# The chained factors of the two hyperbolic layers: a rewritten chain, and a last stage in two groups of tiles

## The chip, the cores and the metric

The kernel runs on one core of one Trainium2 chip. The metric is the device time of one execution in microseconds. An execution was also profiled by the hardware: the profile lists every instruction of the five engines (TensorE: PE for matmuls and PEld for weight loads; VectorE: DVE; ScalarE: ACT; GpSimd: POOL; SyncE: SP, which here only starts DMAs), with start and duration, the program line it comes from, and the names of what it writes and reads. "L720" is line 720 of the program before the change. Times in the profile count from the first instruction.

## The reference

Four graph layers on 3327 nodes with 64 features and a sparse 0/1 matrix `adj`. Each layer normalizes `x`, takes the positive part, and adds its result to `x`. Layers 0 and 3 are the hyperbolic ones. Their core, cut to what matters here:

```python
h = jnp.maximum(_layernorm(x), 0.0)
adj_att = sigmoid(left[:, None] + right[None, :] + b) * adj       # 3327 x 3327
x_local = logmap(h[:, None, :], h[None, :, :], c)                 # mobius_add(-p1, p2), artanh of its norm
support = einsum('ij,ijd->id', adj_att, x_local)
second  = tanh(0.5 * sqrt_c * lambda_x(h, c) * norm(support)) * support / (sqrt_c * norm(support))
res     = mobius_add(h, second, c)                                # num / max(den, 1e-15)
x       = x + where(norm(res) > maxnorm, res / norm(res) * maxnorm, res)
```

`x_local` is never built. All of it lies in the plane of two vectors, so per node the layer's result is `ah * Xr + am * M`: `Xr` is the scaled input row, `M` the row summed over the neighbours, and `ah` and `am` are two numbers per node. They follow from a handful of numbers per node by a long chain of elementwise steps: two square roots, a tanh, two or more divisions. This chain is called the factors below.

Layer 1 is a weighted sum over the last neighbours of each row (counts along a row, exponentials of them, then a product with the features); layer 2 is an attention with two GRU cells.

## The kernel before

**Tiles.** The 3327 nodes are padded to 26 tiles of 128. A number per node is a 128x26 tile, features are 128x26x64. The two halves of the 26 tiles (0 to 12 and 13 to 25) are handled side by side: a chunk `(t, n)` means tiles t to t+n-1 of both halves. `by_tiles(t, c)` is that view of a tile.

**The loops of layers 0 and 3** (`hyperbolic_series`). The columns come in four chunks, `(0, 4), (4, 3), (7, 3), (10, 3)`; each chunk goes over the 26 row blocks, which makes K = 104 steps, two of them to each turn `j` of the loop at L684. A step is: PE products (L611, L612), ACT arctan (L617), ACT sigmoid (L598), POOL times the adjacency (L600), DVE `weights` (L621), PE `sums` (L630, L638). What ends a chunk is put into the dictionary `later` and done in the next turns: `out_of` (ACT copies the sums, L648), `back` (PE transposes them, L657), `to_m` (DVE product for `hm`, L667; ACT square for `mm`, L668) and `to_m2` (DVE sum `M0`, L673; ACT copy to `M`, L674; DVE sum `hm`, L676; then DVE sum `mm`, L677). `M0`, `hm` and `mm` are the numbers per node from which the factors start.

**Order.** ACT, DVE, PE and POOL have their order written out by hand inside a region (L579) that starts before the loop. In layer 0 it stays open until the end of layer 1, so the factors and all of layer 1 run in the order in which they are written. In layer 3 it is closed after the loop (L815); from there a scheduler orders the instructions. SP's DMAs are in the order of their issue.

**After the loop of layer 0**, `plain_decay` begins layer 1. It runs the first count steps of layer 1 (PE counts L1467, ACT exponentials L1473) ahead of the normalization: one of them (`ahead_of_norm(0)`) before `to_m`, one after it, then `e.factors(tp)` (L1620), then eight more. The DVE adds `ah * Xr + am * M` to `X` tile by tile (L1520) and normalizes four groups of tiles (L1525 to L1555), which gives the parts `h` that PE needs for the sums of layer 1 (L1481).

**After the loop of layer 3** all 26 tiles take the factors at once, then `X` is updated in two halves of 13 tiles (L817 to L833): for each half DVE makes two products (L830; the last one is made by ACT tile by tile, L823) and two adds (L831), and `done` starts the half's store (L1956).

**The factors** (`factors`, L713 to L809) are some 63 DVE instructions on 128x26 numbers and one ACT tanh. `root_by_bits` (L122) gives 1/sqrt by a bit trick and three Newton steps of three instructions each. The quotient `1/d` is taken in the middle and multiplied into `am` and `ah` before the second norm. In layer 3 `um` is a lower bound on the tanh's argument.

**The end.** `ok` collects what shows that the fast path may be used: the count of nodes with `x2 >= X2_MIN` (L562, L563) and of adjacency values that are 0 or 1. PE sums it (L2003), DVE turns it into 0 or 1 in `badi` (L2004 to L2006), and every engine loads that number and branches over a slow path (L2007) that isn't taken.

Of the kernel before, what the change touches and what calls it, by code (L numbers as in the profile page):

```python
# [21 lines left out]
P = 128  # L22
# [12 lines left out]
X2_MIN = 22.0  # L35
ARTANH_CLIP = 0.5 * math.log((2.0 - 2.0 ** -23) * 2.0 ** 23)
# [12 lines left out]
def tile_gnn4(ctx: ExitStack, tc: tile.TileContext, x, adjT, att0, b0, w1, bias1, w_gat, a_gat,  # L49
# [72 lines left out]
    def root_by_bits(y, q, src):  # L122

        V.tensor_scalar(y.bitcast(I32), src.bitcast(I32), -0.5, float(0x5f375a86), op0=OP.mult, op1=OP.add)
        for _ in range(3):
            V.scalar_tensor_tensor(q, y, -0.5, y, op0=OP.mult, op1=OP.mult)
            V.tensor_mul(q, q, src)
            V.scalar_tensor_tensor(y, q, 1.5, y, op0=OP.add, op1=OP.mult)
# [171 lines left out]
    def ball(att, b_att, r, min_norm, min_norm2, after=None):  # L300
# [15 lines left out]
        cc, sqc, isqc, um, maxn2 = [const.tile([P, 1], F32, name=n + k) for n in ("cc", "sqc", "isqc", "um", "maxn")]  # L316
        if r is None:
            for t, value in ((cc, 1.0), (sqc, 1.0), (isqc, 1.0), (um, 0.0), (maxn2, min_norm2)):
                V.memset(t, value)
        else:  # L320
# [5 lines left out]
            def of_r():  # L326
                G.tensor_tensor(cc, cc, cc, op=OP.mult)
                for i, (to, src) in enumerate(((cc, cc), (sqc, cc), (isqc, cc))):
                    G.tensor_tensor(to, src, half[:, i:i + 1], op=OP.pow)
                G.tensor_scalar(um, sqc, min_norm / MIN_NORM, None, op0=OP.mult)  # L330
                G.tensor_scalar(maxn2, cc, min_norm2, None, op0=OP.mult)
            after.append(of_r)
        return wlr, bcol, cc, sqc, isqc, um, maxn2

    def hyperbolic_series(r, params, ok, masks=None, done=None, ahead=None, then=None, checks=None):
# [18 lines left out]
        with ExitStack() as st:  # L354
# [8 lines left out]
            wlr, bcol, cc, sqc, isqc, um, maxn2 = params  # L363
# [51 lines left out]
            with room(name="hsp", bufs=1) as tp, room(name="hsps", bufs=2, space=PSUM) as ps, \  # L415
# [136 lines left out]
                for o, (to, on) in enumerate(((junk, V), (pe, A))):  # L552
# [5 lines left out]
                    if o == 0:  # L558
# [3 lines left out]
                        V.scalar_tensor_tensor(good, x2, X2_MIN, nodes, op0=OP.is_ge, op1=OP.mult)  # L562
                        V.reduce_sum(ok, good, axis=AX.X)  # L563
# [96 lines left out]
            def to_m(j, c, slot):  # L660
# [4 lines left out]
                else:  # L665
                    prod = wk.tile([P, 2, 2, 4, D], F32, name="prod", bufs=1)[:, :, :, :c[1], :]
                V.tensor_mul(prod[:, 0], by_tiles(Xr, c), pm)  # L667
                A.activation(prod[:, 1], pm, AF.Square)  # L668
                later[j + 1, 0] = lambda: to_m2(j + 1, c, slot, pm, prod)

            def to_m2(j, c, slot, pm, prod):
                pm0 = slot[:, 1, :c[1] * P].rearrange("p (t i o d) -> p o t i d", i=2, o=2, d=32)
                V.reduce_sum(by_tiles(M0, c), pm0[:, :, :, :, 0], axis=AX.X)  # L673
# [5 lines left out]
            def at(k, first):  # L679

                return tiles[k][0] if 0 <= k < K and tiles[k][1] == 0 and tiles[k][0][0] >= first else None

            sigmoid(0)
            for j in range(-1, K // 2 + (5 if then is None else 1)):  # L684
# [3 lines left out]
                for i in range(2):  # L688
# [13 lines left out]
                    if i == 1 and (j, 1) in later:  # L702
                        later.pop((j, 1))()
                if at(2 * j + 10, 1):
                    columns(at(2 * j + 10, 1))
# [7 lines left out]
            def factors(tp):  # L713

                def new(name):
                    return tp.tile([P, T], F32, name=name)

                def mul(name, a, b):
                    o = new(name)
                    V.tensor_mul(o, a, b)  # L720
                    return o


                k1, k2, bx, bk2, bh, rr = [small[n] for n in ("k", "kb", "bx", "bk", "bh", "rr")]
                stt = V.scalar_tensor_tensor
                V.tensor_scalar(hm, hm, 0.5 * PF, None, op0=OP.mult)

                ca = mul("ca", M0, k2)
                w = mul("w", mm, bk2)
                V.tensor_sub(ca, hm, ca)  # L730
                u = mul("u", bx, hm)
                cx = mul("cx", ca, x2)
                v2 = new("v2")
                V.tensor_add(v2, cx, u)
                vh = new("vh")
                stt(vh, u, 0.5, cx, op0=OP.mult, op1=OP.add)
                V.tensor_mul(v2, v2, ca)
                V.tensor_add(v2, v2, w)
                th, t, a1, d, y2 = [new(n) for n in ("th", "t", "a1", "d", "y2")]
                ah, am = new("ah"), new("am")  # L740


                if r is None:


                    f = MIN_NORM
                    by, g = new("by"), new("g")
                    V.tensor_scalar(by, v2, -f * f, 1.0, op0=OP.mult, op1=OP.add)
                    V.tensor_scalar(g, by, MIN_NORM, None, op0=OP.max)
                    V.reciprocal(g, g)  # L750
                    V.tensor_mul(t, root, g)
                    A.activation(th, t, AF.Tanh)
                    V.tensor_mul(th, th, rr)
                    V.tensor_mul(y2, th, th)
                    stt(vh, vh, 2.0 * f, th, op0=OP.mult, op1=OP.mult)
                    V.tensor_mul(y2, y2, x2)
                    stt(d, v2, f * f, y2, op0=OP.mult, op1=OP.mult)
                else:

                    V.tensor_scalar(t, v2, 1e-8, None, op0=OP.max)  # L760
                    ti, tq = new("ti"), new("tq")
                    root_by_bits(ti, tq, t)
                    V.tensor_mul(t, t, ti)
                    V.tensor_scalar(t, t, um, None, op0=OP.max)
                    A.activation(th, t, AF.Tanh)
                    V.reciprocal(ti, t)
                    ta, th = th, new("th_t")
                    V.tensor_mul(th, ta, ti)
                    V.tensor_mul(y2, th, th)
                    stt(vh, vh, 2.0, th, op0=OP.mult, op1=OP.mult)  # L770
                    V.tensor_mul(y2, y2, v2)
                    V.tensor_mul(d, y2, x2)
                stt(d, d, 1.0, vh, op0=OP.add, op1=OP.add)
                stt(a1, vh, 1.0, y2, op0=OP.add, op1=OP.add)
                V.tensor_scalar(d, d, MIN_NORM, None, op0=OP.max)
                if r is None:
                    stt(ah, a1, f, ca, op0=OP.mult, op1=OP.mult)
                    V.reciprocal(d, d)
                    V.tensor_mul(by, by, th)
                    stt(am, a1, f, bx, op0=OP.mult, op1=OP.mult)  # L780
                    V.tensor_add(ah, ah, by)
                else:
                    V.tensor_mul(th, th, bx)
                    V.reciprocal(d, d)
                    V.tensor_mul(ah, th, ca)
                    V.tensor_mul(am, th, bx)
                    V.tensor_add(ah, ah, a1)
                V.tensor_mul(am, am, d)
                V.tensor_mul(ah, ah, d)

                hm_ = mul("hm_", hm, am)
                n2 = mul("n2", ah, x2)
                V.tensor_mul(am, am, k1)
                V.tensor_add(n2, n2, hm_)
                m2 = mul("m2", mm, am)
                V.tensor_mul(n2, n2, ah)
                V.tensor_mul(m2, m2, am)
                V.tensor_mul(ah, ah, bh)
                V.tensor_add(n2, n2, m2)
                if r is not None:  # L800
                    V.tensor_scalar(am, am, isqc, None, op0=OP.mult)
                V.tensor_scalar(n2, n2, maxn2, None, op0=OP.max)
                ns, nq = new("ns"), new("ns_q")
                root_by_bits(ns, nq, n2)
                n2 = ns
                V.tensor_scalar(n2, n2, 1.0 - 0.004, 1.0, op0=OP.mult, op1=OP.min)
                V.tensor_mul(am, am, n2)
                V.tensor_mul(ah, ah, n2)
                return ah, am  # L809

            if then is not None:
                then(SimpleNamespace(Xr=Xr, M=M, slots=slots, later=later, factors=factors, close=lp.close,
                                     ahead=ahead, close_all=hs.close))
                return
            region.close()  # L815
            lp.close()
            with room(name="hse", bufs=1) as tp:  # L817
                ah, am = factors(tp)
                last = HALVES[1]
                extra = tp.tile([P, T // 2, D], F32, name="extra")  # L820
                for k in range(T // 2):
                    t = last.start + k
                    A.activation(extra[:, k, :], M[:, t, :], AF.Copy, scale=am[:, t:t + 1])  # L823
                for ts in HALVES:
                    for a, b in ((Xr, ah), (M, am)):
                        if ts is last and a is M:
                            prod = extra
                        else:
                            prod = tp.tile([P, T // 2, D], F32, name="prod", bufs=2)
# [1223 lines left out]
```

## Time and profile before

| what | value |
|---|---|
| median of three runs (lowest to highest) | 730.57 us (729.93 to 732.24) |
| the profiled execution: its own time, and its span | 730.23 us, 728.5 us |
| busy share of the span: PE, DVE, ACT, POOL | 87%, 74%, 74%, 59% |
| mean granted TensorE clock | 0.961 of full speed |
| DMA | 119.25 MB, 164 GB/s over the span |
| chain that ended last, by engine | PE 64%, DVE 12%, issue 6%, POOL 6%, ACT 5%, DMA 4% |

The busy shares are means over stages with different limits. The chain that ended last is followed back from the last instruction: at each step to what released it, or to the instruction before it on its engine. The span runs from the first to the last instruction; about 1.7 us of the execution's own time lie outside it.

### The profile page before, as it was taken

To read this page: it belongs to the slowest core of one execution; us is meant where nothing else is said; L and a number is where in the kernel's file an instruction comes from. 1 tells how busy PE (TensorE), PEld (TensorE's weight loads), DVE (VectorE), ACT (ScalarE), POOL (GpSimd) and SP (SyncE) were. 2 spreads that over 40 slices of the span, in tenths; PEclk is the share of its full clock that TensorE was granted. 3 is DMA by queue.
4 is the path that set the end of the run, shared out by engine and by line. 5 is a ranking of instruction groups with operands and counts; after the bars stand their busy time and mean duration, and the time that the engine had idled before them with its cause. 6 is when DMAs were issued, how large, how long until landed. Compare 5 with 4: busy or idle time off the path is not lost.

```text
span 728.5 us, 11966 instructions
## 1 busy us (share of the span) xinstructions
PE 632.3 (87%) x4227; PEld 256.4 (35%) x4227; DVE 542.6 (74%) x999; ACT 536.7 (74%) x691; POOL 430.8 (59%) x326
## 2 busy tenths in 40 slices
PE   0899999999999798989998997169999999999940
PEld 0622233333333243434445642042223333333310
DVE  6867778777787799999645339887667877777656
ACT  2688888888888785687871586258888889888831
POOL 2699999989999202116620000048887887888820
PEclk9999999999999999999999999579999999999985
DMA  3988898898888706489940000203334444444001
GB/s 63 334 259 279 263 274 256 279 298 261 267 260 273 274 26 226 132 289 358 403 162 2 1 1 1 94 19 93 94 94 133 115 117 138 120 118 116 2 3 50
DMA packets 61494, 119.25 MB, mean 164 GB/s; under 512 B 9552, under 2 KB 33776, under 8 KB 61424
## 3 DMA queue, kind: packets, MB, share of 16 engines
q1 hardware_dynamic: 57072, 118.38, 51.1%
q10 hardware_dynamic: 4352, 0.02, 0.3%
q8 instruction: 35, 0.57, 0.3%
q14 instruction: 35, 0.29, 0.1%
HBM read 115.64 MB, written 0.88 MB: 160 GB/s over the span
## 4 chain that ended last, share of the span: by engine, by line
PE 64%; DVE 12%; issue 6%; POOL 6%; ACT 5%; DMA 4%; SPq 1%; ACTq 1%; POOLq 0%; DVEq 0%
PE slot L630 16%; PE slot L638 9%; PE slot L611 9%; PE slot L1467 8%; PE slot L612 7%; POOL sig L600 6%; PE slot L1766 5%; PE slot L1481 5%; DMA adj<-in 3%; ACT sig L598 2%; PE slot L1882 1%; DVE X L1520 1%; ACTq L307 1%; DMA own<-in 1%; DVE sig L621 1%
## 5 line engine op out<-in xcount | busy, mean ns | idle before, releaser
L621 DVE SCALAR_TENSOR_TENSOR sig<-slot,sig 128x768 f32<-128x768 f32 (+1 forms) x208 | 212.7, 1023 | 105.7 <-POOL sig L600 105.6
L617 ACT ACTIVATE slot<-slot 128x768 f32<-128x768 f32 (+1 forms) x208 | 177.3, 853 | 53.3 <-PE slot L612 53.0
L600 POOL TENSOR_TENSOR sig<-adj,sig 128x768 f32<-128x768 f32 (+1 forms) x104 | 201.1, 1960 | 14.5 <-ACT sig L598 11.5
L598 ACT ACTIVATE sig<-leftB,right 128x768 f32<-128x768 f32 (+1 forms) x208 | 203.3, 977 | 0.1
L600 POOL TENSOR_TENSOR sig<-mask,sig 128x768 f32<-128x768 fp8e4 (+1 forms) x104 | 173.2, 1678 | 40.5 <-ACT sig L598 35.1
L630 PE MATMUL slot<-sig,Xr 128*64 128x384 f32 (+1 forms) x832 | 169.3, 526 | 5.8 <-DVE sig L621 5.7
L611 PE MATMUL slot<-XC,XT 128*128 128x384 f16 (+1 forms) x416 | 142.2, 342 | 3.1 <-ACT sum L648 1.7
L612 PE MATMUL slot<-XF,XE 73*128 73x384 f16 (+1 forms) x416 | 141.4, 340 | 0.0
L638 PE MATMUL slot<-sig,X 128*32 128x384 f32 (+1 forms) x832 | 94.2, 525 | 0.0
L1473 ACT ACTIVATE w<-slot,ebias 128x832 bf16<-128x832 f32 x76 | 69.0, 952 | 26.3 <-PE slot L1467 25.9
L630 PEld LDWEIGHTS slot<-sig,Xr 128*64 128x64 f32 x832 | 49.8, 135 | 87.1 <-issue 62.0
L611 PEld LDWEIGHTS <-XT 128*128 128x128 f16 x416 | 40.7, 98 | 93.8 <-issue 67.4
L1467 PE MATMUL slot<-mask,rest 128*128 128x416 fp8e4 x208 | 53.9, 341 | 5.7 <-ACT adj L1473 3.5
L1467 PE MATMUL slot<-mask,after 128*128 128x416 fp8e4 x208 | 53.4, 339 | 1.3 <-DVE deg L1491 1.3
L612 PEld LDWEIGHTS <-XE 73*128 73x128 f16 x416 | 40.7, 98 | 29.5 <-issue 5.4
L1362 DVE TENSOR_SCALAR_CACHE_REDUCE same<-late 128x832 fp8e4<-128x832 f32 x48 | 48.4, 1009 | 0.0
L204 POOL TENSOR_TENSOR mask<-mask,offdiag 128x128 fp8e4<-128x128 fp8e4 x26 | 16.5, 645 | 46.1 <-PE slot L1467 46.1
L421 POOL MEMSET X<- 128x832 f32 x2 | 1.6, 792 | 69.4 <-DVE o L1911 69.4
L1766 PE MATMUL slot<-mask,own 128*64 128x416 fp8e4 x416 | 39.8, 346 | 2.2 <-DVE deg L1491 2.2
L638 PEld LDWEIGHTS slot<-sig,X 128*32 128x32 f32 x832 | 16.4, 108 | 67.7 <-issue 66.1
L1481 PE MATMUL slot<-w,h 128*64 128x416 bf16 x304 | 34.0, 345 | 0.0
L527 PE MATMUL pt<-ident_h,Xp 128*64 128x128 f16 x32 | 2.6, 313 | 35.5 <-ACT Xp L466 35.5
(323 smaller groups left out, 681.0 us busy)
## 6 DMA issues: line engine op xcount, KB each, us to landing
adj<-in SPq DMA_DIRECT2D x78, 384.0 KB, 4.8
late<-in SPq DMA_DIRECT2D x48, 416.0 KB, 3.2
adj<-in SPq DMA_DIRECT2D x17, 832.0 KB, 8.4
adj<-in SPq DMA_DIRECT2D x27, 512.0 KB, 5.1
ahead<-in SPq DMA_DIRECT2D x14, 832.0 KB, 6.4
ahead<-in SPq DMA_DIRECT2D x16, 416.0 KB, 5.6
own<-in SPq DMA_DIRECT2D x16, 416.0 KB
own<-in SPq DMA_DIRECT2D x8, 832.0 KB
```

The lines of the kernel that those rows point to most:

```text
L598: A.activation(sig, leftB[c], AF.Sigmoid, bias=right[:, b:b + 1])
L600: G.tensor_tensor(sig, adj, sig, op=OP.mult)
L611: PE.matmul(L[:, o, :c[1] * P], XT[:, rows], XC[c][:, o, :], start=True, stop=False)
L612: PE.matmul(L[:, o, :c[1] * P], XE[:KE, rows], XF[c][:, o, :], start=False, stop=True)
L617: A.activation(L, L, AF.Arctan, scale=PA / SX ** 2)
L621: V.scalar_tensor_tensor(sig, slot[:, :, :tiles[k][0][1] * P], PC, sig, op0=OP.add, op1=OP.mult)
L630: PE.matmul(acc[c][o * D:(o + 1) * D, 0, :n], Xr[:, b, :], sigs[k][:, o, :], start=b == 0, stop=b == T - 1)
L638: PE.matmul(acc[c][q:q + 32, 1, :n], X0[:, b - 1 + i, :], w[:, o, :], start=b == 1, stop=b == T - 1, tile_position=(0, q))
L1467: PE.matmul(cnt[o][:, h, :BK], w, cols(k, o, h), start=w is after and steps[k][1] == T - 1, stop=True, skip_group_check=True)
L1473: A.activation(ws[k][:, o, :, :], cnt[o][:, :, :BK], AF.Exp, scale=-LN2, bias=ebias)
L1481: PE.matmul(acc[c][o * D:(o + 1) * D, h, :BK], parts[i][:, b, :], w[:, o, h, :], start=b == T - 1 and i == 0, stop=b == 0 and i == 1)
L1766: PE.matmul(acc[k][o * D:(o + 1) * D, :], w, mask[:, o * HP + k * BK:o * HP + (k + 1) * BK], start=n == 0 and i == 0, stop=n == T - 1 and ...
```

## The change

1. **The chain is rewritten** for both layers. `root_by_bits` takes one third-order step and one Newton step in place of three Newton steps (8 instructions, before 10); constants are left out of the steps and multiplied in later (`ROOT`). The scaling of `hm` by 0.5·PF goes into the instructions that use it. `1/d` is no longer multiplied into `am` and `ah` before the second norm; the norm's bound is multiplied by `d` squared instead (`dd`), and `1/d` is taken as the upper bound of the last factor. In layer 3 the lower bound `um` is applied to the square (`um2`, with 1e-8 in it), so the tanh's argument needs no bound of its own and no reciprocal.
2. **The factors become a generator** that gives way after each instruction and works on a chunk's view. Layer 0 runs it to the end on all 26 tiles (`all_factors`). In layer 3 it runs once for the chunk `(0, 10)` of 20 tiles, "early", and once for the chunk `(10, 3)` of the last 6 tiles, "late". Eight early steps are written after each of the two `sigmoid` places of turn `j = K // 2`, where the loop has no more steps for DVE: 16 in all. The rest alternates with the late steps, one by one, and after the early factors the 20 tiles' X update takes their turn; then comes the late X update. The intermediate numbers lie in a part of a load buffer of the loop (`checks.adjs[2]`).
3. **The X update** (`moves`) lets ACT scale all of `M` in place, tile by tile, and DVE scale `Xr` in place and do both adds, in pieces of 5 tiles (early) and 3 tiles (late). `store_tiles` stores 20 tiles, then 6; each store takes two blocks of a partition.
4. The region of the written-out order now ends after all of this.
5. In `to_m` the DVE sum `M0` is written directly after the product, ahead of ACT's square, for every chunk of both layers.
6. A second condition, `x2 <= X2_MAX`, is one more DVE instruction in the preparation of both loops.

```diff
-    def root_by_bits(y, q, src):
+    def root_by_bits(y, q, r, src):
         V.tensor_scalar(y.bitcast(I32), src.bitcast(I32), -0.5, float(0x5f375a86), op0=OP.mult, op1=OP.add)
-        for _ in range(3):
-            V.scalar_tensor_tensor(q, y, -0.5, y, op0=OP.mult, op1=OP.mult)
-            V.tensor_mul(q, q, src)
-            V.scalar_tensor_tensor(y, q, 1.5, y, op0=OP.add, op1=OP.mult)
+        V.tensor_mul(q, y, y)
+        V.tensor_mul(q, q, src)
+        V.scalar_tensor_tensor(r, q, 10.0 / 3.0, q, op0=OP.subtract, op1=OP.mult)
+        V.scalar_tensor_tensor(y, r, 5.0, y, op0=OP.add, op1=OP.mult)
+        V.scalar_tensor_tensor(q, y, -0.5 * ROOT ** 2, y, op0=OP.mult, op1=OP.mult)
+        V.tensor_mul(q, q, src)
+        V.scalar_tensor_tensor(y, q, 1.5, y, op0=OP.add, op1=OP.mult)
...
                         V.scalar_tensor_tensor(good, x2, X2_MIN, nodes, op0=OP.is_ge, op1=OP.mult)
+                        V.scalar_tensor_tensor(good, x2, X2_MAX, good, op0=OP.is_le, op1=OP.mult)
...
                 V.tensor_mul(prod[:, 0], by_tiles(Xr, c), pm)
+                V.reduce_sum(by_tiles(M0, c), pm0[:, :, :, :, 0], axis=AX.X)
                 A.activation(prod[:, 1], pm, AF.Square)
...
             def to_m2(j, c, slot, pm, prod):
-                V.reduce_sum(by_tiles(M0, c), pm0[:, :, :, :, 0], axis=AX.X)
                 A.activation(by_tiles(M, c), pm, AF.Copy)
...
+            def factors(place, c):
...
+                mul(ca, m0c, k2)
+                stt(u, hmc, 0.5 * PF, bx, op0=OP.mult, op1=OP.mult)
+                stt(ca, hmc, 0.5 * PF, ca, op0=OP.mult, op1=OP.subtract)
...
+                    V.tensor_scalar(t, v2, um2, None, op0=OP.max)
+                    yield from root_by_bits(ns, nq, nr, t)
+                    mul(t, t, ns)
+                    A.activation(th, t, AF.Tanh, scale=ROOT)
+                    stt(th, th, ROOT, ns, op0=OP.mult, op1=OP.mult)
...
+                stt(dd, d, maxn2, d, op0=OP.mult, op1=OP.mult)
...
+                V.reciprocal(d, d)
+                add(n2, n2, m2)
+                V.tensor_max(n2, n2, dd)
+                mul(ah, ah, bh)
...
+                yield from root_by_bits(ns, nq, nr, n2)
+                stt(ns, ns, ROOT * (1.0 - 0.004), d, op0=OP.mult, op1=OP.min)
+                mul(ah, ah, ns)
+                mul(am, am, ns)
+                return ah, am
...
+            def place_in_loop(name):
+                return checks.adjs[2][:, len(places) * T:(len(places) + 1) * T]
...
+            def moves(c, pieces):
+                ah, am = found[c]
...
+                for os, ts in cut:
+                    for o in range(os.start, os.stop):
+                        for t in range(ts.start, ts.stop):
+                            m = by_tiles(M, c)[:, o, t, :]
+                            A.activation(m, m, AF.Copy, scale=am[:, o, t:t + 1])
+                for os, ts in cut:
+                    x, a = by_tiles(X, c)[:, os, ts], by_tiles(Xr, c)[:, os, ts]
+                    scaled(a, ah[:, os, ts], ts)
+                    V.tensor_add(x, x, a)
+                for os, ts in cut:
+                    x, m = by_tiles(X, c)[:, os, ts], by_tiles(M, c)[:, os, ts]
+                    V.tensor_add(x, x, m)
+                done(c)
+
+            def both(one, two):
+                for _ in one:
+                    next(two, None)
...
+                    if j == K // 2:
+                        for _ in range(8):
+                            next(moving, None)
...
+            def of_early():
+                yield from moving
+                yield from moves(early, [(o, 1, t, 5) for o in range(2) for t in (0, 5)])
+
+            rest = of_early()
+            both(of_tiles(late_), rest)
+            for _ in rest:
+                pass
+            for _ in moves(late_, [(0, 1, 0, 3), (1, 1, 0, 3)]):
+                pass
             region.close()
             lp.close()
-            with room(name="hse", bufs=1) as tp:
-                ah, am = factors(tp)
...
+    def store_tiles(c):
+        ts = slice(c[0], c[0] + c[1])
+        nc.sync.dma_start(out.rearrange("p (h t d) -> p h t d", h=2, d=D)[:, :, ts, :], X2[:, :, ts, :])
```

In the diff the `yield` after each instruction of the generators is left out. A `yield` is where a generator gives way to the other; `value_of` runs one to its end.

## The prediction

> **What bounds the kernel now.** I read the page first (PE 87% busy, PE 64% of the chain that ended last), then the table by stage, because the change touches two stages in which PE is not the limit. Its columns: stretch and length in us, busy us and count of PE, PEld, DVE, ACT, POOL, granted clock, DMA share, GB/s.
>
> ```profile
> 500.00:697.00 197.00, 195.57 (x1212) 68.68 (x1210) 145.76 (x206) 171.53 (x211) 162.97 (x100) 1.00 0.36 101
> 697.00:704.30 7.30, 3.97 (x32) 1.26 (x24) 2.53 (x6) 1.86 (x4) 0.89 (x1) 1.00 0.00 0
> 704.30:715.20 10.90, 0.00 (x0) 0.00 (x0) 9.76 (x67) 0.27 (x2) 0.00 (x0) 0.55 0.02 5
> 715.20:722.40 7.20, 0.00 (x0) 0.00 (x0) 6.93 (x8) 3.17 (x13) 0.00 (x0) 0.50 0.16 61
> 722.40:728.50 6.10, 0.00 (x0) 0.00 (x0) 0.00 (x0) 0.00 (x0) 0.00 (x0) 0.50 0.20 75
> ```
>
> The second loop is PE's (195.6 of 197.0 us). From 704.3 to 722.4 DVE works alone: 10.9 us of factors, 7.2 us of X update; then 6.1 us in which no engine computes. In the factors, the timeline of DVE (start, duration) has two prices:
>
> ```profile
> 704.46 0.18 DVE L720 TENSOR_TENSOR w<-mm,bk 128x26 f32<-128x26 f32 x1
> 704.55 0.18 DVE L720 TENSOR_TENSOR u<-bx,hm 128x26 f32<-128x26 f32 x1
> ...
> 706.20 0.19 DVE L126 SCALAR_TENSOR_TENSOR tq<-ti 128x26 f32<-128x26 f32 x1
> 706.42 0.19 DVE L127 TENSOR_TENSOR tq<-tq,t 128x26 f32<-128x26 f32 x1
> ```
>
> Independent neighbours start 0.10 us apart, dependent ones 0.22. Going through the old chain with these two prices (0.13 more for a reciprocal, 0.05 for a scalar read from a tile) gives 8.71 us for layer 0's factors, where 249.47 to 258.32 = 8.85 were measured; in layer 3 10.8 for 10.97. So I trust it to 3%.
>
> In layer 0 the factors lie beside PE work, so I asked for the waits from 240 to 300 us (total, times, longest):
>
> ```profile
> PE slot L1481 <- DVE h L1553: 1.9, 1, 1.9
> ...
> PE slot L1481 <- DVE h L1555: 0.4, 1, 0.4
> ```
>
> PE stands 2.3 us for the normalized rows of the second group, which DVE reaches at 275.4 to 276.6 after the factors without one pause. So layer 0's factors are on the path too.
>
> **Layer 0, step by step.** The timeline where its factors begin:
>
> ```profile
> 246.27 0.55 DVE L667 TENSOR_TENSOR same<-Xr,slot 128x384 f32<-128x384 f32 x1
> 248.46 0.17 DVE L673 TENSOR_REDUCE M<-slot 128x6 f32<-128x12 f32 x1 [1.64 <-ACT same L668]
> 248.55 0.55 DVE L676 TENSOR_REDUCE hm<-same 128x6 f32<-128x384 f32 x1
> 249.01 0.55 DVE L677 TENSOR_REDUCE mm<-same 128x6 f32<-128x384 f32 x1
> ```
>
> - `M0` (L673) goes behind L667 and `hm` (L676) follows; only `mm` still needs ACT's square, which ends at 248.43. It starts at 248.47, not 249.01: **-0.54**.
> - Up to the tanh's product: the scaling of `hm` goes (0.10), the new order gives back 0.04: -0.06.
> - From that product to the root, 3.41 us before (252.17 to 255.58): the reciprocal (0.35) and two products by `d` leave the chain; `dd` and the maximum enter beside it. By the two prices 2.91: **-0.50**.
> - The root: 8 dependent links, before 10: 2 x 0.22 = **-0.44**. At the end `ah` comes ahead of `am`: -0.10.
>
> Together -1.64: the first L1520 starts at 256.68. PE's wait is long enough to take it: ACT's tanh, which stood 1.1 us for DVE in front of exponentials that PE needs, comes 0.6 us earlier, so PE is earlier by 0.6 and still waits 2.3 - 1.64 + 0.6 = 1.3. After that PE is busy 100.3 of 102.6 us (276.6 to 379.2). **What is late next** is the adjacency: from 345 to 370 DMA moves 400 GB/s and DVE's masks stand for it 4.9 us. But the last mask is made at 368.6, PE takes its block after 375, and the loads are started by DVE's own masks, which move too. I take -1.64; bounds -0.9 (the links gain only their issue) and -1.8.
>
> **The preparation of loop two** gets one instruction between L562 (487.79) and L563 (488.00), dependent on both sides: **+0.21**, since DVE goes straight on to copies for which PE and POOL stand. In the first preparation DVE idles 0.39 us behind it (before 30.28), which hides it; without that cover 0.21 too.
>
> **`to_m` of the six other chunks**: ACT loses a wait of 0.24 us (L674 on L673); PE, 99% busy, hides it. I take 0; bounds -0.4 and 0.1.
>
> **Layer 3.** All of this is DVE in order.
> - 16 early steps start at 698.9, when L621 is done, and end at 701.5. PE's transposes release DVE at 702.16, so they cost nothing; without this cover 2.6.
> - `mm` starts 0.45 earlier than 703.82 (as above, with ACT's square 0.09 later behind `M0`). Factors go from **703.83**.
> - 40 pairs of a late step (128x6) and an early one (128x20). A 128x4 operation takes 0.07 us of issue and a chain of 128x9 goes at 0.20, so a pair is two issues, 0.16, or one dependent step, 0.20: mean 0.19, so 7.6; each of the two tanhs stalls DVE some 0.35 us: **8.3**.
> - Late steps 41 to 52 alternate with 12 pieces of 128x320. From 0.10 for 26 columns and 0.95 for 832 (715.25 to 716.20) a piece takes 0.42, the small one beside it 0.07: **5.9**. ACT's 20 scalings at 0.24 (the 13 of L823) run beside it, 4.8 us, ahead of the adds that need them.
> - Late steps 53 to 56: **0.65**. Six operations of 128x192 at 0.28, two of them dependent, plus the last one's end: **1.95**. L2004 to L2006, 0.3 in a row, fall partly into DVE's waits: **0.15**. 3% of my pricing's shortfall on the chain: **0.3**.
>
> Sum 17.25: the last add ends at 721.1, before at 722.33: **-1.25**. Bounds: +0.5 (pairs at 0.23) and -2.0. That interleaving works is seen in layer 1, where an X update alternates with a chain:
>
> ```profile
> 262.12 0.28 DVE L1520 SCALAR_TENSOR_TENSOR X<-Xr,ah,X 128x64 f32<-128x64 f32 x1
> 262.31 0.16 DVE L1540 TENSOR_SCALAR ln_y<-ln_v 128x4 int32<-128x4 int32 x1
> 262.38 0.28 DVE L1520 SCALAR_TENSOR_TENSOR X<-Xr,ah,X 128x64 f32<-128x64 f32 x1
> ```
>
> The small one takes 0.07 us, although L1520 writes another slice of one tile each time.
>
> [...]The row says 0.10 between independent starts at a duration of 0.18, so the row decides.
>
> **The tail after DVE.** SP starts the last store at 722.41 (0.34 us), loads the verdict and branches:
>
> ```profile
> L2007 SPq EVENT_SEMAPHORE  x8: 17/17/17, 726.1 to 726.7; - x8
> ...
> L2007 SPq TENSOR_LOAD <-badi x1: 521/521/521, 722.8 to 722.8; - x1
> L2007 SPq COMPARE_BRANCH  x1: 50/50/50, 723.4 to 723.4; - x1
> ```
>
> From 723.4 to 726.1 SP is silent; POOL (706.0 to 708.6) and ACT (716.1 to 718.7) show the same 2.6 us behind their branch with nothing stored. [...]But the branch, not the store, ends last: 0. A store of two blocks takes 0.54 us to issue on SP, as the two-block loads here (one-block ones 0.33): **+0.2**. The first store (655 KB, issued near 718.8; the old first store moved at 353 GB/s in its best microsecond, so 1.9 us) is written out by 721, before the last is issued.
>
> **Sum**: -1.64 + 0.21 - 1.25 + 0.2 = **-2.5**; 730.23 of the profiled execution goes to 727.7. The median lies 0.34 above that execution, so **728.1**.
>
> **Rivals.**
> - *Only one part pays* (12%). Layer 0 alone (the tail is bound by DVE's issue, as its 93% in 704 to 722 suggests, though those are overlapping durations): 730.57 - 1.43 = 729.1. Or the tail alone (the DMA stretch swallows layer 0's gain): 729.7, against which the 6 us of margin speaks.
> - *DVE doesn't overlap* (5%), place: the 52 pairs from 703.8. [...]It decides from a pair of 0.25: 40 x 0.06 eats the 2.5. The overlapped starts speak against it.
> - *More* (15%): L674's wait, the checks and the tanh stalls cost nothing: 1.0 less, 727.1.
>
> **Numbers.** The forecast, 728.1 with its own range 727.1 to 729.0, has 68%. 0.3% (2.2 us, about what a measurement tells from no change) is at 728.4, inside it: 47 faster, 21 same. With the rivals: faster 0.62, same 0.33, slower 0.05. Range 726.9 to 729.6.
>
> **What would show it.** First L1520 near 256.7; PE's wait for L1553 near 1 us; 16 small operations between 698.9 and 702.2; pairs about 0.2 us apart; last add near 721; from it to the end 6.4 us. It is wrong if pairs take 0.4, if the late adds stand for the first store, or if PE's start at 276.7 doesn't move.

## The result and the profile after

The changed kernel takes 727.28 us (median of 8 runs, 725.84 to 729.33); before, in the same comparison, took 732.38 (729.93 to 734.18). The ratio is 0.9936, 95% interval 0.9916 to 0.9956: 4.7 us less, 3.2 to 6.2 by the interval. The forecast was 2.5 less. The profiled execution takes 726.02 (span 724.3; before 730.23 and 728.5).

The table by stage of the changed kernel (stretch and length in us, busy us and count of PE, PEld, DVE, ACT, POOL, granted clock, DMA share, GB/s):

```profile
496.60:693.60 197.00, 195.78 (x1215) 68.87 (x1213) 146.11 (x207) 171.91 (x211) 163.76 (x100) 1.00 0.35 101
693.60:700.46 6.86, 3.93 (x32) 1.26 (x24) 4.97 (x22) 1.75 (x4) 0.86 (x1) 0.98 0.00 0
700.46:708.70 8.24, 0.00 (x0) 0.00 (x0) 8.07 (x83) 0.43 (x2) 0.00 (x0) 0.50 0.02 6
708.70:717.30 8.60, 0.00 (x0) 0.00 (x0) 8.38 (x35) 6.42 (x26) 0.00 (x0) 0.50 0.15 58
717.30:724.30 7.00, 0.00 (x0) 0.00 (x0) 0.00 (x0) 0.00 (x0) 0.00 (x0) 0.50 0.17 58
```

The loop is PE's as before. The second stretch now holds 22 DVE instructions where before had 6: the 16 early steps lie in DVE's pause. DVE then works 16.8 us without PE, where the old kernel took 18.1, but the tail without an engine has grown from 6.1 to 7.0.

In layer 0, the timeline of DVE in the changed kernel:

```profile
246.58 0.55 DVE L684 TENSOR_TENSOR same<-Xr,slot 128x384 f32<-128x384 f32 x1
247.04 0.16 DVE L685 TENSOR_REDUCE M<-slot 128x6 f32<-128x12 f32 x1
247.16 0.55 DVE L692 TENSOR_REDUCE hm<-same 128x6 f32<-128x384 f32 x1
248.77 0.55 DVE L693 TENSOR_REDUCE mm<-same 128x6 f32<-128x384 f32 x1 [1.06 <-ACT same L686]
...
256.97 0.48 DVE L1633 SCALAR_TENSOR_TENSOR X<-Xr,ah,X 128x64 f32<-128x64 f32 x2
```

From the product to the first X update 10.39 us; before 12.05 (246.27 to 258.32). PE's waits for the rows that follow:

```profile
PE slot L1594 <- DVE h L1666: 0.9, 1, 0.9
...
PE slot L1594 <- DVE h L1668: 0.4, 1, 0.4
```

1.3 us in all, 2.3 before.

**Where 4.2 us of the two profiled executions went.** I matched PE's matmuls of both traces one by one. After is 0.31 us late at the end of the first loop and 1.33 early after layer 0's factors (a step of -1.65), and stays at -1.33 to the end of layer 1. There comes a step of -1.62, at the second preparation +0.22, in the second loop three of -0.23, and in what follows its last DVE product -0.80. The step of -1.62 is the clock. Both kernels let PE stand there for 2.24 us; before:

```profile
382.34:384.58 2.24, 0.00 (x1) 0.00 (x0) 2.16 (x4) 0.43 (x2) 0.00 (x0) 1.00 0.00 0
384.58:388.00 3.42, 3.42 (x17) 2.33 (x17) 0.00 (x0) 0.00 (x0) 0.00 (x0) 0.51 0.02 5
```

and after:

```profile
381.01:383.25 2.24, 0.00 (x1) 0.00 (x0) 2.16 (x4) 0.43 (x2) 0.00 (x0) 1.00 0.00 0
383.25:386.67 3.42, 3.42 (x34) 2.44 (x35) 0.98 (x2) 0.00 (x0) 0.00 (x0) 1.00 0.02 5
```

The same pause, but 17 matmuls in the next 3.42 us at a granted clock of 0.51 (half clock, below), or 34 at 1.00. Whether the change does this, what the steps inside the loop are, and what the interleaving is worth, can't be read from these two traces alone.

### The profile page after: what moved, and what is told of

It is laid out like the page before. It is cut to its first block, busy times and chain, and to the rows that moved or that the text cites. A ratio compares the mean times of both kernels' runs of the same rounds, so it can differ in the third digit from the quotient of the medians.

```text
span 724.3 us, 12042 instructions
## 1 busy us (share of the span) xinstructions
PE 628.6 (87%) x4227; PEld 253.2 (35%) x4227; DVE 543.4 (75%) x1055; ACT 539.4 (74%) x705; POOL 430.3 (59%) x326
## 4 chain that ended last, share of the span: by engine, by line
PE 64%; DVE 16%; POOL 5%; issue 4%; DMA 4%; ACT 3%; SPq 2%; ACTq 1%; POOLq 0%; DVEq 0%
PE slot L646 18%; PE slot L654 10%; PE slot L627 9%; PE slot L628 8%; PE slot L1580 6%; PE slot L1879 5%; POOL sig L616 5%; PE slot L1594 4%; DMA adj<-in 3%; DVE same L1475 2%; PE slot L1995 1%; ACT sig L614 1%; DVE mask L1563 1%; DVE sig L637 1%; DVE X L1633 1%
## 5 line engine op out<-in xcount | busy, mean ns | idle before, releaser
L637 DVE SCALAR_TENSOR_TENSOR sig<-slot,sig 128x768 f32<-128x768 f32 (+1 forms) x208 | 212.6, 1022 | 110.6 <-POOL sig L616 109.4
```

The source lines that it names most:

```text
L637: V.scalar_tensor_tensor(sig, slot[:, :, :tiles[k][0][1] * P], PC, sig, op0=OP.add, op1=OP.mult)
```

## The experiments

Each kernel was timed beside the kernel before; the ratio (95% interval) is to that. Since the first loop (207.1 to 210.7 us in the 14 profiles) and the clock (half at one place in 9 of them) vary from run to run, the columns on the right are the firmer evidence: the second loop from its first DVE product to its last, from there to the last add, and on to the end of the span (us, from one profile each).

| kernel | median us | ratio to before | loop 2 | to last add | tail | half clock at the end of layer 1 |
|---|---|---|---|---|---|---|
| before | | | 206.27 | 24.41 | 6.17 | yes |
| changed | 727.28 | 0.9936 (0.9916, 0.9956) | 205.62 | 22.75 | 7.03 | no |
| again | 727.48 | 0.9945 (0.9919, 0.9970) | 205.60 | 22.75 | 6.85 | no |
| chain_alone | 724.83 | 0.9911 (0.9887, 0.9935) | 205.60 | 21.79 | 5.99 | yes |
| m0_alone | 730.88 | 0.9982 (0.9962, 1.0002) | 205.58 | 23.70 | 5.97 | yes |
| in_turn | 733.07 | 1.0014 (1.0000, 1.0028) | 205.62 | 27.30 | 7.07 | yes |
| one_block | 728.30 | 0.9955 (0.9938, 0.9972) | 205.61 | 22.76 | 6.37 | no |
| early_in_loop | 738.91 | 1.0100 (1.0074, 1.0125) | 218.73 | 19.40 | 6.88 | yes |
| both_parts | 738.31 | 1.0092 (1.0067, 1.0117) | 219.45 | 19.39 | 6.32 | yes |
| chain_again | 726.54 | 0.9920 (0.9893, 0.9946) | 205.61 | 21.77 | 6.00 | yes |
| chain_act | 725.49 | 0.9908 (0.9884, 0.9932) | 205.61 | 21.13 | 6.14 | yes |
| m0_last_only | 728.63 | 0.9955 (0.9939, 0.9971) | 206.29 | 22.74 | 6.99 | no |
| chain_no_test | 724.89 | 0.9902 (0.9868, 0.9935) | 205.58 | 21.79 | 6.13 | no |
| m0_last_again | 729.38 | 0.9974 (0.9959, 0.9989) | 206.30 | 22.76 | 6.84 | yes |

### The changed kernel again: is the clock its doing?

> The changed kernel once more, nothing edited. At the end of layer 1 PE stood 2.24 us for DVE in both first profiles (before from 382.34, after from 381.01), and behind it the granted clock was 0.50 until 388 in before and 1.00 in after; this alone moved PE 1.62 us. Theory A: that clock is not the change's doing. Then this profile may show either value, its PE is 1.6 us later there if it shows 0.50, and the median of all runs of the changed kernel stays 726 to 729. Rival B: the change keeps the clock up, by where it puts the pause. Then this profile shows 1.00 again, and every kernel with the same layer 0 does.

The full clock again, which both allowed. The next kernels decide: chain_alone and in_turn have the same instructions up to there and show the half clock, and m0_last_only and m0_last_again, one and the same kernel, show one of each. In all, 9 of the 14 profiles show it and 5 do not, with a pause of 2.24 us in each. So B falls: here it is chance, and the 1.62 us are not the change's.

What goes with it can be read from the same traces. All changes of the granted clock in one trace lie on a grid of 3.41 us (in before at 384.65, 388.06, 452.91, 483.63 and 705.50, which are 1, 19, 9 and 65 steps apart; in the changed kernel at 450.98, 481.70 and 700.16, 9 and 64 apart), and this grid lies differently against the program in each run. In the 9 profiles with the half clock, 1.77 to 2.24 us of the pause fall into one step of the grid; in the 5 others, at most 1.71. The two nearest cases, each with the step that holds most of the pause and the one after it, are chain_again:

```profile
381.05:384.47 3.42, 1.65 (x14) 0.64 (x13) 3.39 (x5) 0.93 (x2) 0.00 (x0) 1.00 0.01 2
384.47:387.88 3.41, 2.94 (x15) 1.81 (x15) 0.42 (x2) 0.00 (x0) 0.00 (x0) 0.50 0.02 5
```

and the changed kernel:

```profile
379.30:382.72 3.42, 1.71 (x14) 0.64 (x13) 3.39 (x5) 0.93 (x2) 0.00 (x0) 1.00 0.01 2
382.72:386.13 3.41, 2.88 (x28) 2.09 (x29) 0.92 (x3) 0.00 (x0) 0.00 (x0) 1.00 0.02 5
```

So at this place the half clock followed a step with 1.77 us or more of the pause in it, in the nearest case with PE busy for 1.65 of 3.42, and the clock stayed full with 1.71 of the pause and 1.71 of work, about half of the step each.

By this reading the change does act on the clock at another place. Behind layer 0's factors PE waits 2.3 us in before and in m0_alone, and in m0_alone the half clock followed:

```profile
275.29:278.71 3.42, 1.14 (x9) 0.48 (x10) 3.25 (x8) 0.95 (x1) 0.00 (x0) 1.00 0.96 324
278.71:282.12 3.41, 3.41 (x14) 1.12 (x13) 3.24 (x17) 0.95 (x1) 0.00 (x0) 0.50 0.92 324
```

In before two steps share the pause, with PE busy for 1.97 us (272.01 to 275.42) and 2.53 (275.42 to 278.83), and the clock stayed full. In m0_alone PE was 1.28 us later than in before until then, 2.86 later afterwards, and made up 0.73 by 340. In these two traces 68% of the grid's possible positions would give such a step there, with PE busy for less than half of it. In the twelve traces with the new chain, where PE waits 1.3 us, no position would (in the changed kernel's, PE is busy for 2.1 us or more of the step, wherever the grid lies). My estimate from these busy times and shifts is 0.68 x (1.58 - 0.73), some 0.6 us that the change saves on average. The timed runs fit: the mean granted clock is 0.959 in 38 runs of before and in 14 of m0_alone, and 0.961 in 17 of the changed kernel, where one step at half clock lowers it by 0.0023. No kernel was run to test it.

### The chain without the interleaving

```diff
-            rest = of_early()
-            both(of_tiles(late_), rest)
...
+            with room(name="hse", bufs=1) as tp:
+                ah, am = all_factors(tp)
...
-    hyperbolic_series(r3, params3, ok[:, 2:3], masks, store_tiles, checks=Late(zo))
+    hyperbolic_series(r3, params3, ok[:, 2:3], masks, store, checks=Late(zo))
```

> The change without the interleaving: the new chain, M0 moved and the added test of x2 stay; layer 3 ends as before, 26 tiles at once, X in two halves, two stores of one block. Theory A (my sums): the new chain for 26 tiles is 57 links, 8.8 us by the two prices and 9.1 with the 3% they fell short; from mm 0.45 earlier it gives the first X update some 8.7 us after mm, the update takes 7.08 as before and 6.17 follow. Against the second loop's last DVE product (697.92 in before, its end of span 30.6 later) the end is then 28.3 us later, where the changed kernel took 29.8: it is FASTER than the changed kernel by about 1.5 us, and the interleaving costs more than it saves. Rival B: the interleaving pays as the sum of the prediction had it; then this kernel ends 31 us or more after that product and is slower than the changed one by 1 us or more.

A. From the last product to the end 27.78 us (28.3 expected), in the repeat 27.77; the changed kernel took 29.78 and 29.60. Its table by stage from `mm` on:

```profile
704.66:713.85 9.19, 0.00 (x0) 0.00 (x0) 8.14 (x59) 0.55 (x2) 0.00 (x0) 0.52 0.03 5
713.85:721.00 7.15, 0.00 (x0) 0.00 (x0) 6.91 (x8) 3.21 (x13) 0.00 (x0) 0.50 0.16 62
721.00:726.90 5.90, 0.00 (x0) 0.00 (x0) 0.00 (x0) 0.00 (x0) 0.00 (x0) 0.50 0.20 78
```

The first step of its chain, four from the middle and the 41st, in DVE's timeline:

```profile
704.44 0.17 DVE L716 TENSOR_TENSOR ca<-M,kb 128x26 f32<-128x26 f32 x1
...
709.20 0.18 DVE L788 TENSOR_TENSOR am<-th,bx 128x26 f32<-128x26 f32 x1
709.29 0.18 DVE L790 TENSOR_TENSOR y<-y,v 128x26 f32<-128x26 f32 x1
709.41 0.19 DVE L792 TENSOR_TENSOR ah<-am,ca 128x26 f32<-128x26 f32 x1
709.51 0.18 DVE L794 SCALAR_TENSOR_TENSOR a<-vh,y 128x26 f32<-128x26 f32 x1
...
711.03 0.12 DVE L822 TENSOR_TENSOR m<-m,am 128x26 f32<-128x26 f32 x1
```

and a stretch of the changed kernel:

```profile
701.65 0.18 DVE L784 TENSOR_TENSOR late<-late 128x20 f32<-128x20 f32 x1
701.75 0.16 DVE L728 SCALAR_TENSOR_TENSOR late<-late 128x6 f32<-128x6 f32 x1
701.82 0.17 DVE L786 SCALAR_TENSOR_TENSOR late<-late 128x20 f32<-128x20 f32 x1
701.91 0.16 DVE L730 TENSOR_TENSOR late<-late 128x6 f32<-128x6 f32 x1
701.99 0.17 DVE L788 TENSOR_TENSOR late<-late,bx 128x20 f32<-128x20 f32 x1
```

In these stretches both start an instruction every 0.07 to 0.12 us. The one chain does it alone, since its order already puts independent strands side by side there, and each of its starts serves all 26 tiles. (In the steps of its roots, each of which needs the one before, it starts one every 0.22 us.) So 40 pairs take 8.2 us, while the one chain's first 40 steps take 6.1 (704.44 to 711.03, less 0.46 for the `mm` in it): 2.1 lost. The late 16 steps beside the pieces, with the late move, take 8.6; the one chain's last 16 with its X update 9.9 (711.03 to 720.93): 1.3 won. With 0.2 more in front of the first step, the interleaved kernel is 0.96 behind at the last add, and 0.9 to 1.0 more in the tail.

### Late behind early

```diff
-            both(of_tiles(late_), rest)
             for _ in rest:
                 pass
+            for _ in of_tiles(late_):
+                pass
```

> The changed kernel, with the late six tiles' factors issued behind the early twenty's factors and X update, not between them. Theory A: in the interleaving each hides in the other's stalls: alone, the remaining 40 early steps take 6.5 us, the 12 pieces 4.8 and the late 56 steps 8.1, together 19.4 where the interleaved stretch took 14.8: slower than the changed kernel by 4 to 5 us. Rival B: DVE's time for an instruction does not overlap with its neighbour, so that order is nothing to it: the same to 1 us.

A: 34.4 us from the last product to the end, 4.6 more. Alone the early 40 steps take 5.8 us, the 12 pieces 5.4, and the late chain 8.05, each within 0.7 of what was expected. The late chain's first step and the X update behind it:

```profile
713.14 0.16 DVE L716 TENSOR_TENSOR late<-M,kb 128x6 f32<-128x6 f32 x1
...
721.19 0.36 DVE L870 TENSOR_TENSOR Xr<-Xr,late 128x192 f32<-128x192 f32 x1
```

So the interleaving does hide 4.5 us, of a second chain and of a cut-up X update that the one chain does not have.

### M0 moved, and nothing else; and M0 moved in all but six chunks

```diff
                 V.tensor_mul(prod[:, 0], by_tiles(Xr, c), pm)
+                V.reduce_sum(by_tiles(M0, c), pm0[:, :, :, :, 0], axis=AX.X)
                 A.activation(prod[:, 1], pm, AF.Square)
...
             def to_m2(j, c, slot, pm, prod):
-                V.reduce_sum(by_tiles(M0, c), pm0[:, :, :, :, 0], axis=AX.X)
                 A.activation(by_tiles(M, c), pm, AF.Copy)
```

> The kernel before, with M0's sum moved in front of ACT's square for all eight chunks and nothing else. Theory A: the three steps of 0.23 us that PE gained inside the second loop of the changed kernel (at the three boundaries between its chunks) come from this move: PE is 0.6 to 0.7 us nearer to the loop's start at its end than in before, here too, with the old chain; layer 0's factors start 0.5 us earlier against the last DVE product of loop one, layer 3's 0.4. In all 1.6 to 2.3 us less than before, if the clock is equal. Rival B: these steps are chance in PE's records or the clock, as my forecast of 0 had it: the second loop is as long as before to 0.1 us, and the whole gains at most 1.0.

```diff
-                V.reduce_sum(by_tiles(M0, c), pm0[:, :, :, :, 0], axis=AX.X)
+                if c == chunks[-1]:
+                    V.reduce_sum(by_tiles(M0, c), pm0[:, :, :, :, 0], axis=AX.X)
                 A.activation(prod[:, 1], pm, AF.Square)
...
+                if c != chunks[-1]:
+                    V.reduce_sum(by_tiles(M0, c), pm0[:, :, :, :, 0], axis=AX.X)
                 A.activation(by_tiles(M, c), pm, AF.Copy)
```

> The changed kernel, with M0's sum put back behind ACT's square for the six chunks that are not the last of their loop (ACT waits for DVE's sum there again). Theory A: these six moves pay, which the prediction had at 0: the second loop, from its first DVE product to its last, is 0.69 us longer again (206.27 as in before, where the changed kernel took 205.62), in the first loop up to as much, less where the adjacency's loads set its length. Slower than the changed kernel by 0.7 to 1.4 us. Rival B: the gain in the second loop came from elsewhere (fewer instructions at the loop's end, other buffers): it stays at 205.6 to 205.7.

> The changed kernel with M0's sum back behind the square for the six chunks that are not the last of their loop, once more. The first loop took 207.1 and 207.3 us (first DVE product to last) in the two profiles with that old place, and 207.8 to 210.7 in all those with the new one, while adjacency loads landed late. Theory A: that is the chance of the loads; this profile may lie anywhere from 207 to 210.7. Rival B: the new place costs the first loop 1 to 3 us, since PE runs into the loads; then this profile shows 207.1 to 207.4 again, the second loop 206.3, and the timed median is 1 us or more under the changed kernel's 727.3 to 727.5.

The second loop settles it: 206.27, 206.29 and 206.30 us with the old place, 205.58 to 205.62 in every other kernel whose loop is otherwise the same. ACT's waits in that loop, m0_last_only:

```profile
ACT slot L633 <- PE slot L628: 26.5, 45, 1.2
ACT M L693 <- DVE M L692: 0.7, 3, 0.2
```

and the changed kernel, where this is the only row:

```profile
ACT slot L633 <- PE slot L628: 26.8, 48, 1.2
```

ACT's three waits of 0.24 us reach PE in full. Moved alone, `M0` also gave layer 0 its 0.54 (from +1.81 against before to +1.27) and the end 0.91 (29.67 for 30.58); the timed gain, 1.3 us (-0.1 to 2.8), lies under the 2.1 of these three and under the 1.6 to 2.3 expected, but its interval holds both.

The first loop took 207.1 and 207.3 us in the first two profiles with the old place and 207.8 to 210.7 in eleven with the new, which looked like a price. The repeat took 208.3 us with the old place: outside B's 207.1 to 207.4, but still below ten of the eleven. The timed runs speak against a price: both kernels with the old place have medians of 728.6 and 729.4, above the changed kernel's, where a price of 1 us or more would put them below it. In chain_alone, whose first loop took 210.7, an adjacency load issued at 139.30 landed at 147.23, 7.9 us later, and POOL stood 2.2 us until then.

### The last store in two blocks of one

```diff
-        nc.sync.dma_start(out.rearrange("p (h t d) -> p h t d", h=2, d=D)[:, :, ts, :], X2[:, :, ts, :])
+            nc.sync.dma_start(out.rearrange("p (t d) -> p t d", d=D)[:, o:o + c[1], :], X[:, o:o + c[1], :])
```

> The changed kernel, its last store (six tiles, two blocks of three in each half of X) cut into two stores of one block, the first issued when its half's last add is done. From last add to the end the kernels with one-block stores took 5.97 to 6.17 us, those with the two-block store 6.81 to 7.05. Theory A: the two-block form costs this: its issue takes SP 0.575 instead of 0.343, and SP's load of the flag behind it 0.99 instead of 0.52. Then SP's load takes 0.52 here, and the end comes 6.0 to 6.3 after the last add: 0.7 to 0.9 less in all than the changed kernel. Rival B: the load is slow because stores are just under way, whatever their form; two issues in a row then make it no better: 6.8 to 7.1, the load at 0.9 or more.

A by the row, though the gain is a little under the 0.7 to 0.9 expected. SP's load of the verdict behind the last store, changed kernel (durations in ns, min/median/max):

```profile
L2124 SPq TENSOR_LOAD <-badi x1: 990/990/990, 718.0 to 718.0; - x1
```

and one_block:

```profile
L2131 SPq TENSOR_LOAD <-badi x1: 513/513/513, 720.7 to 720.7; - x1
```

The tail is 6.37 (6.0 to 6.3 expected), 0.5 to 0.7 less than the changed kernel's. The medians (728.3 for 727.3 and 727.5) don't show the gain; this profile's first loop took 210.2 us, 1.2 more than the changed kernel's.

### Early factors inside the loop

```diff
-                    if j == K // 2:
-                        for _ in range(8):
-                            next(moving, None)
+                    for _ in range(steps.get((j - K // 2, i), 0)):
+                        next(moving, None)
```

> The changed kernel with the early 20 tiles' factors moved into the second loop's last six steps (3 to 5 instructions of DVE behind each of its products, the tanh too), part of their X update in DVE's pause behind the loop, and the rest at places where the late factors' chain stands for itself. Theory A: in the interleaved stretch a pair takes 0.20 us, while one chain of 26 tiles takes 0.146 a step: the pairing hides little, since the chain's neighbours are half independent already; what counts is how many instructions stand after the loop. DVE has 0.9 us free beside each product there. So the loop ends as before to 0.5 us, and from its last product to the last add it takes 18.5 to 19.7 us, where the changed kernel took 22.75 and the chain alone 21.8: 3 to 4 us less than the changed kernel. Rival B: DVE's free time there is cover that the loop needs; PE's end of the loop is 2 us or more later, and the whole gains under 1 us or loses.

> The two edits together: early factors in the loop, last store as two of one block. Theory A of both: the gains add, 3.7 to 4.9 us less than the changed kernel, that is 722 to 724. Rival B: nothing adds, since SP's branch or the early store's landing sets the end instead; within 0.5 us of the early factors in the loop alone.

B for the first text, and worse than B had it: both kernels are 11 to 12 us slower than the changed one. What stands after the loop is as short as A said (19.4 us to the last add; with the two one-block stores the tail is 0.56 shorter, so at the end these gains add), but the loop takes 13.1 us more, or 13.8 with both edits. Its timeline:

```profile
685.11 3.11 POOL L616 TENSOR_TENSOR sig<-mask,sig 128x768 f32<-128x768 fp8e4 x2 [0.53 <-ACT sig L614]
685.41 1.30 DVE L728 SCALAR_TENSOR_TENSOR late<-late 128x20 f32<-128x20 f32 x1
...
692.96 1.57 POOL L616 TENSOR_TENSOR sig<-mask,sig 128x768 f32<-128x768 fp8e4 x1 [1.70 <-ACT sig L614]
...
693.14 1.42 DVE L138 SCALAR_TENSOR_TENSOR late<-late 128x20 f32<-128x20 f32 x1
694.59 0.18 DVE L140 TENSOR_TENSOR late<-late 128x20 f32<-128x20 f32 x1
```

L138 takes 1.42 us instead of 0.18 and ends at 694.56, when POOL's product ends (694.53). Nine of the early instructions in the loop do this, 10.3 us beyond 0.18 each: DVE's free time there was not free. I had counted pauses, not what else may run in them. The rest of the 13.1 us was not taken apart; the granted clock was also half from 692.96 to 696.37 and from 703.20 to 706.61.

### ACT scales more of M; the test of x2 left out

```diff
-                for k in range(T // 2):
-                    t = last.start + k
-                    A.activation(extra[:, k, :], M[:, t, :], AF.Copy, scale=am[:, t:t + 1])
+                for k in (*range(own, T // 2), *range(last.start, T)):
+                    A.activation(extra[:, k, :], M[:, k, :], AF.Copy, scale=am[:, k:k + 1])
```

```diff
-                        V.scalar_tensor_tensor(good, x2, X2_MAX, good, op0=OP.is_le, op1=OP.mult)
```

> The chain alone once more, nothing edited, beside the next three. Theory A: it is the faster kernel (ratio to before 0.991 again, 0.989 to 0.994), with 27.8 us from the second loop's last DVE product to the end of the span (before 30.6, changed 29.6 to 29.8). Rival B: its 724.8 was a lucky median; now its ratio is that of the changed kernel, 0.994 to 0.996.

> The chain alone, with ACT scaling 20 of the 26 tiles of M by the factor instead of 13; DVE scales the other 6 in one product of 128x384. Theory A: DVE sets that end (seven operations of 128x832 at 0.95 to 1.05); one of them shrinks to half, so the last add ends 0.45 to 0.5 us earlier after the factors than the 7.1 of the chain alone, and the whole is 0.5 less. ACT's 20 at 0.24 take 4.8 us and end 1.2 us ahead of the last add's start. Rival B: the last add waits for ACT, whose first scaling starts late; 0 or some tenths more than the chain alone.

> The chain alone without the added test of x2 against 1e12 (the part left out is that guard of the normal path; the data lie far below). Theory A: the second preparation is shorter by its 0.21 to 0.22 us on PE, as it got longer by 0.22 in the changed kernel; the first one not at all, since DVE pauses behind it. Rival B: its place is taken by another wait in the second preparation; the same to 0.1.

Theory A in all three. The repeat of the chain alone has 27.77 us behind the last product. With 20 tiles on ACT the last add comes 0.64 to 0.66 earlier, a little more than expected. Without the test, PE leaves the second preparation 0.22 earlier against chain_again (-0.65 before it, -0.87 behind). chain_act, which keeps the test of `x2`, is faster than the kernel before and than the changed one: 725.5 us, ratio 0.9908 against the changed kernel's 0.9936 and 0.9945. The intervals overlap; what carries it is that the four kernels with the single chain have ratios of 0.9902 to 0.9920, all below every other, and that their traces are at least 1.6 us shorter than the changed kernel's at the end.

## Why the prediction was right, step by step

The time, its sign and its range were right. By steps without chance in them the trace gives -1.65 + 0.22 - 0.67 and, at the end, -0.80 to -0.98 (29.78 and 29.60 for 30.58): about **-3.0**, where the sum had -2.5. Part of this is luck. In the sum, misses of -0.67 and -0.41 are partly undone by one of +0.5 to +0.7. And the time came out within 0.8 us of 728.1 because two errors cancel: the forecast started from three runs of before with the median 730.57, 1.8 below the eight of the comparison, and the change was 2.2 larger than forecast.

- **Layer 0, -1.64: -1.65.** `mm` begins 2.19 us after the product, before 2.74: -0.55 (forecast -0.54). Behind it the four parts are -0.08, -0.50, -0.44 and -0.10, forecast -0.06, -0.50, -0.44 and -0.10. chain_alone and in_turn show the same step (-1.64). PE's wait is 1.3, as forecast, and the shift lasts to layer 1's end: the adjacency was not late next.
- **The added instruction, +0.21: +0.22**, and gone when it is left out.
- **`to_m` of the six other chunks, 0: wrong.** It was -0.67 in the second loop, outside my bound of -0.4. The step that failed is "PE, 99% busy, hides it": ACT's three waits reached PE in full. Being busy for nearly all of the stretch (195.57 of 197.00 us), PE had next to no pause of its own in which to take them up. In the first loop it can't be seen beside the loads.
- **Layer 3 to the last add, -1.25: -1.66.** The 16 early steps are hidden: the last of them ends at 698.16, before the product that waits for PE. `mm` -0.41 for -0.45; pairs 8.2 us for 8.3; the 12 pieces 5.9 for 5.9; the last move 2.07 for 1.95. The 0.15 for the checks and the 0.3 of shortfall weren't needed, as they fall inside the pairs. The end of the early steps:

```profile
697.98 0.18 DVE L138 SCALAR_TENSOR_TENSOR late<-late 128x20 f32<-128x20 f32 x1
698.74 0.56 DVE L684 TENSOR_TENSOR prod<-Xr,slot 128x384 f32<-128x384 f32 x1 [0.57 <-PE slot L673]
```

- **What I credited was wrong, though the sum was right.** The prediction said "That interleaving works". It hides 4.5 us, but the one chain alone ends 1.9 us earlier. I set the interleaved kernel only against the old chain, never the new chain against itself.
- **The tail, +0.2: +0.68 to +0.86.** I priced the store's issue and took the load of the verdict behind it at its old 0.52; it takes 0.99 behind a two-block store. This uses up what DVE gained in layer 3: m0_alone, with the old chain there, has 29.67 us after the last product, the changed kernel 29.78 and 29.60.
- **Rivals.** DVE without overlap is excluded: the 40 pairs take 8.2 us, some 0.2 each, where the durations of the two instructions in one, 0.17 and 0.16 in the changed kernel's stretch above, add up to 0.33. The 5% that I gave this rival was my estimate. "More", where single terms cost nothing, came nearest in the time: L674's wait fell away (-0.67) and the checks added nothing to the pairs, while the tail took 0.5 to 0.7 back.
- **What the sum did not have: the clock.** The medians moved 4.7 us (3.2 to 6.2; 4.0 in the repeat), the steps give 3.0. By the estimate above, some 0.6 of the rest is the half clock behind layer 0 that the shorter wait avoids. What remains stays open; the half clock at the end of layer 1 and the loads of the first loop are large enough for it, but how often each falls in timed runs wasn't measured.

## What to carry to other kernels

Before interleaving two copies of a chain, write down what the chain alone costs after it was shortened: here its order already filled part of the gaps, and the split doubled the starts, which lost 2.1 us to win 1.3. PE, busy 99% of the second loop, paid in full for each of ACT's three waits of 0.24 us in front of it (the loop was 0.67 longer with them), so a reduction moved ahead of another engine's operation was worth its wait. And a pause of an engine is room only for instructions that nothing else in that moment shuts out: nine that I put into DVE's pauses took 10.3 us beyond 0.18 each.

## What the runs showed of the hardware that I had not expected

- A DVE instruction with two SBUF operands stood for POOL's running product, nine times in the loop of early_in_loop: 128x20 in up to 1.54 us instead of 0.18, ending within 0.04 us of POOL's. DVE's products L637, one of whose operands is in PSUM, take a median of 0.96 beside it. Whether the place of the operands is what counts, no run tested.
- After one and the same pause of PE, 2.24 us, the granted clock was half for 3.41 us in 9 profiles and full in 5, 1.6 us of PE's time. In these 14 it went with the place of the pause on a grid of 3.41 us: half after a step in which PE was still busy for 1.65 us, full after one with 1.71.
- SP's load of one word took 0.97 to 0.99 us right behind a store of two blocks (six profiles) and 0.50 to 0.53 behind one of one block (eight).
